# Deformable attention and a bottleneck block on one core: what the first and the last image do around the main loop

## The chip, the cores and the metric

The kernel runs on one core of a Trainium2 chip. The core has five engines that run side by side, each with its own list of instructions: TensorE (PE, matrix products), VectorE (DVE), ScalarE (ACT), GpSimd (POOL) and SyncE (SP, which here only issues transfers). They meet at semaphores. Data lies in SBUF (128 partitions), products go to PSUM, and 16 DMA engines move data from and to memory. Every number is float32. The metric is the device time of one execution in microseconds (us), as the median of several runs.

## What is computed

The input `x` holds 8 images of 512 channels and 64 by 64 pixels. Two layers follow each other, each behind a group norm over 32 groups and each added to its input.

Layer 0 is attention with deformed sampling. In the names of the reference, cut to what matters:

```
q   = w_q x                                   # 512 x 512, all 4096 pixels
t   = gelu(q[every 4th row and column] * w_off1 + b_off1)
off = tanh(w_off2 t) * 4                      # where to sample, per group of channels
kv_feats = bilinear samples of q at grid + off    # 16 x 16 = 256 positions
k, v = split(w_kv kv_feats)
out  = softmax(q k / 8) v                     # 8 heads of 64, 4096 queries, 256 keys
x    = x + w_out out + b_out
```

Layer 1 is a bottleneck: a 1x1 convolution from 512 to 32 channels, a depthwise 3x3 convolution of stride 2 (to 32 x 32), two dense layers over the 1024 pixels (to 256 and back), a depthwise 3x3 transposed convolution back to 64 x 64, and a 1x1 convolution to 512 channels, added to its input.

## The kernel before

**Tiles and buffers.** An image is 8 tiles (`NT`) of 512 pixels; a tile holds 4 blocks (`NCC`) of 128 channels. Two images lie in SBUF in turn. PSUM has eight banks of 128 x 512: two pairs in `ps_s` (tag `s`), two single banks that take turns in `ps_mm` (tag `mm`), and one bank each of tags `pa` and `pn` in `ps_a`. When a tile takes a bank, its first product waits until the last reader of the tile that had the bank is done. The order of instructions of each engine is the order in which the Python code issues them (a manual schedule); generators are advanced by hand, so that pieces of one image's work stand between pieces of another's.

**First images.** Image 0 is loaded, its statistics are taken (`norm_x`, L199), and `keep_up` (L1194) puts products on PE that nothing reads. `norm_q` turns the statistics into a scale and a shift: `group_stats` sums over groups with two small products (`gps`, L171, and `gpsb`, L180), each in a bank of `ps_mm`, VectorE and GpSimd finish the scale (L182, L183), and `normalise` (L212) applies it. The first tile's blocks go to VectorE (`t == 0`) or ScalarE, those of the second to GpSimd. `project_q` (L248) makes the query projection of one image, tile by tile, in the seven products of a Strassen-like scheme (L277): sums of weights are kept in the still unused buffers `wout` and `kt`, and the query is also turned into pixel-major form (`by_pixel`: transposes L326, copies L334 or L336, a write to memory on SP's queue, L337). The last tile's four transposes use the banks `pa`, `mm`, `pn`, `mm`. `activate` (L296) leaves gelu values for the offsets in the block `wout[:, 3]` and in a small tile. While image 0 is projected, image 1's statistics are taken between the pieces (L1210 to L1213), and its `group_stats` fall into the last tile of image 0 (L1212).

Then image 1's query projection runs beside the sampling of image 0 (`samples[0]`). `sample` (L421) begins with the offset products (L428, 16 small ones in a bank of `mm`) and a tanh (L437); VectorE works out the positions, GpSimd gathers rows of the pixel-major query (L523), and PE turns the weighted samples back to channels (L497). At the end of that come, in this order (L1222 to L1230):

```
while next(other) != LATE:
    pass
project_k(0, mqs.pop(0), wkv[0])
drain(other)
rest.pop(1)()
logits(*names[0])
next(samples[1])
load_wout()
project_v(0, wkv[1])
```

`project_k` makes the keys (L537, copied by ScalarE in L544), `drain(other)` is the four transposes of image 1's last tile, `rest.pop(1)` two maxima on VectorE (L288), `logits` the first products of query and keys with their exponentials (L584, L592), `next(samples[1])` image 1's offset products and tanh, `load_wout` the load of the output weights on SP's queue, which overwrites the block the offset products read, and `project_v` the values (L564, copied in L571). Until `logits` takes them, the four tiles `es4` hold the key and value weights of image 0 (`wkv`).

**Main loop.** A round `g` (L1231) is one pair of heads of one tile: the values weighted by the exponentials (`weighted_values`, L602), every second round the sum of the exponentials (L629), the logits of round `g + 1`, and, six rounds behind (`LAG`), one block of the output projection (`project_out`, L671). `fill` (L1237) advances the work beside it: the sampling and projections of the next image and layer 1 of the one before. From round 5 of image 0 on it also advances `samples[1]`. Reciprocals of the sums (`invert`, L642) are moved between partitions by SP (L648) and scale the result (`scale_two`, L651).

**Last image.** Behind the last round there is nothing to put beside, so layer 1 of image 7 runs alone (L1289 to L1316). `diag` holds diagonal matrices, made by ScalarE (L1297), with which PE computes some of the depthwise taps. `last_tile` (L755) takes the statistics and the 1x1 convolution (L737) block by block. `layer1` (L813) then goes from engine to engine: ScalarE and VectorE move the result to SBUF (L835, L837), the nine taps of the depthwise convolution go to VectorE (five, L881 and L883) and PE (four, L877), VectorE adds both (L879), two transposes (L889) with their copy (L892), the first dense layer (L900, L908, L914, L923), the second (L934, L947), the transposed convolution on PE (L984) beside VectorE (`upsample`), and the output products (L1007), to which the image is added (L1094); each 128 x 512 block is stored by SP (L1097).

Of the kernel before, what the change touches and what calls it, by code (L numbers as in the profile page):

```python
# [8 lines left out]
F32 = mybir.dt.float32  # L9
# [7 lines left out]
P = 128  # L17
B = 8
C = 512
NCC = C // P  # L20
# [29 lines left out]
def kernel(  # L50
# [111 lines left out]
    def group_stats(st, which, b):  # L162

        nm = f"{which}_{b}"
        mv = small.tile([P, NCC, 2], F32, tag="mv", name=f"mv{nm}")
        for cc in range(NCC):
            nc.vector.bn_aggr(mv[:, cc, :], st[:, cc].rearrange("p t s -> p (t s)"))
        mean, var = mv[:, :, 0], mv[:, :, 1]
        yield None
        gps = ps_mm.tile([P, TP], F32, tag="mm", name=f"gps{nm}")  # L170
        nc.tensor.matmul(gps[:, :NCC], cst[:, K_GRP : K_GRP + P], mean, start=True, stop=True)  # L171
        gs = small.tile([P, 2, NCC], F32, tag=f"gs{which}", name=f"gs{nm}")
        nc.vector.tensor_copy(gs[:, 0], gps[:, :NCC])
        dv = small.tile([P, NCC], F32, tag="dv", name=f"dv{nm}")
        nc.vector.tensor_sub(dv, mean, gs[:, 0])
        nc.vector.tensor_mul(dv, dv, dv)
        nc.vector.tensor_add(dv, dv, var)
        yield None
        gps2 = ps_mm.tile([P, TP], F32, tag="mm", name=f"gpsb{nm}")
        nc.tensor.matmul(gps2[:, :NCC], cst[:, K_GRP : K_GRP + P], dv, start=True, stop=True)  # L180
        ve = small.tile([P, NCC], F32, tag="ve", name=f"ve{nm}")
        nc.vector.tensor_scalar_add(ve, gps2[:, :NCC], EPS)  # L182
        nc.gpsimd.tensor_tensor(gs[:, 1], ve, nhalf, ALU.pow)  # L183
        return gs
# [22 lines left out]
    def norm_q(b, st, norms):  # L207
# [4 lines left out]
        def normalise(t, cc):  # L212
            xc, scale = x_tile(b, t)[:, cc, :], gs[:, 1, cc : cc + 1]
            if t == 1 or t == 0 and (b or cc < 2):
                (nc.vector, nc.gpsimd)[t].tensor_scalar(
                    xc, xc, gs[:, 0, cc : cc + 1], scale, ALU.subtract, ALU.mult
                )
            else:
                nc.scalar.activation(  # L219
                    xc, xc, AF.Identity, bias=shift[:, cc : cc + 1], scale=scale  # L220
                )
# [466 lines left out]
    def attention_max(b, t):  # L688

        qt = q_tile(b, t)  # L690
        for hp in range(NCC):
# [41 lines left out]
            nc.scalar.copy(qt[:, hp, :], pa)  # L733

    def convolve(b, py, cw, h, cc):
        for rb in range(4):
            nc.tensor.matmul(  # L737
                py[rb * CB : (rb + 1) * CB, :],
                cw[:, cc, :],
                out_tile(b, 2 * rb + h)[:, cc, :],  # L740
                start=(cc == 0),
                stop=(cc == NCC - 1),
            )
# [69 lines left out]
    def layer1(b, st, project, place, v, conv=None, diag=None):  # L813
# [13 lines left out]
        if conv:  # L827
            nc.vector.memset(y[:, :, 0:1], 0.0)
            nc.vector.memset(y[0:CB, 0:1, :], 0.0)
            py, pb = conv()  # L830
            nc.vector.tensor_sub(yb, col(V_CONVB), pb)
            for h in range(2):
# [39 lines left out]
        for k in range(9):  # L872
            ki, kj = divmod(k, 3)
            yk = y[:, ki : ki + 15 : 2, kj : kj + 63 : 2]
            w = col(V_DWW + k)
            if diag and k > 4:
                nc.tensor.matmul(pd, diag[V_DWW + k], yk, start=(k == 5), stop=(k == 8))  # L877
                if k == 8:
                    nc.vector.tensor_add(z, z, pd)  # L879
            elif k == 0:  # L880
                nc.vector.tensor_scalar(z3, yk, w, col(V_DWB), ALU.mult, ALU.add)  # L881
            else:
                nc.vector.scalar_tensor_tensor(z3, yk, w, z3, ALU.mult, ALU.add)  # L883
# [4 lines left out]
        for h in range(2):  # L888
            nc.tensor.transpose(pz[:, h * P : (h + 1) * P], z[:, h * P : (h + 1) * P], ident)  # L889
        o += NK  # L890
        zT = wflat[:, o : o + 2 * P].rearrange("p (h c) -> p h c", h=2)
# [5 lines left out]
        for k in range(8):  # L897
# [7 lines left out]
                stop=(k >= 4),  # L905
            )
        parts4 = z
        nc.scalar.copy(parts4, ph[:, : 2 * P])  # L908
# [4 lines left out]
        for oc in range(2):  # L913
# [5 lines left out]
                stop=True,  # L919
            )  # L920
        hT = small.tile([P, 2, CB], F32, tag="hT", name=f"hT_{b}")
        for oc in range(2):
# [7 lines left out]
        for n0, n, rbs in ((0, NK, 4), (NK, 32, 3)):  # L930
            for oc in range(2):
                for rb in range(rbs):
# [6 lines left out]
                        stop=(oc == 1),  # L939
                    )  # L940

        o += 2 * P
# [230 lines left out]
    with tc.manual_schedule():  # L1173
# [11 lines left out]
        load_weights_late()  # L1185
        st = new_stats(0, 0)
        drain(norm_x(0, st))

# [4 lines left out]

        def keep_up(n):  # L1194
            for _ in range(n):
                nc.tensor.matmul(idle, ident, x_tile(0, NT - 2)[:, 0, :], start=True, stop=True)

        keep_up(5)
        steps = norm_q(0, st, norms)
# [5 lines left out]
        drain(steps)  # L1205
        keep_up(2)

# [14 lines left out]
        while next(other) != LATE:  # L1222
            pass
        project_k(0, mqs.pop(0), wkv[0])
        drain(other)
        rest.pop(1)()
        logits(*names[0])
        next(samples[1])
        load_wout()
        project_v(0, wkv[1])  # L1230
        for g in range(len(names)):  # L1231
# [29 lines left out]
            else:  # L1261
                if summed:
                    invert(*names[g - 1])
                if g + 1 < len(names):
                    logits(*names[g + 1])
            if g % 2:
                scale_two()
# [26 lines left out]
        diag = {}  # L1294
        for i, w in enumerate([V_DWW + k for k in range(5, 9)] + [V_DEW + k for k in (0, 1, 2, 6, 7, 8)]):
            diag[w] = es4[i // 8][:, i // 4 % 2, i % 4 * P : (i % 4 + 1) * P]
# [138 lines left out]
```

## Time and profile before

| | |
|---|---|
| median of three runs | 3271.72 us (3270.57 to 3271.77) |
| the profiled execution's own time | 3273.27 us |
| its span, first to last instruction | 3271.5 us |
| mean granted clock of TensorE | 0.995 of full speed |
| busy of PE, DVE, ACT, POOL | 98%, 71%, 36%, 19% of the span |
| chain of work that ended last | PE 95%, DVE 3%, issue 1%, ACT 1% |
| keys of image 0 on PE (L537) | 261.3 to 268.4 us |
| first round of the main loop on PE (L602) | 285.34 us |
| last convolution of image 7 on PE (L737) | ends at 3223.6 us |
| first output block summed (L1094) | 3242.47 us |

An execution is recorded by the hardware profiler. Its page gives the busy time of every engine, the span in 40 slices with the clock that TensorE was granted, the chain of work that ended last, and the groups of instructions by line (L277 is line 277 of the kernel). The trace answers further questions: who waited for whom, instructions in order of time, and busy time by stretch. Matrix products are pipelined, and their ends are modelled.

### The profile page before, as it was taken

To read this page: it belongs to the slowest core of one execution; us is meant where nothing else is said; L and a number is where in the kernel's file an instruction comes from. 1 tells how busy PE (TensorE), PEld (TensorE's weight loads), DVE (VectorE), ACT (ScalarE), POOL (GpSimd) and SP (SyncE) were. 2 spreads that over 40 slices of the span, in tenths; PEclk is the share of its full clock that TensorE was granted. 3 is DMA by queue.
4 is the path that set the end of the run, shared out by engine and by line. 5 is a ranking of instruction groups with operands and counts; after the bars stand their busy time and mean duration, and the time that the engine had idled before them with its cause. 6 is when DMAs were issued, how large, how long until landed. Compare 5 with 4: busy or idle time off the path is not lost.

```text
span 3271.5 us, 46349 instructions
## 1 busy us (share of the span) xinstructions
PE 3216.1 (98%) x18270; PEld 1536.2 (47%) x18270; DVE 2322.9 (71%) x3779; ACT 1189.5 (36%) x1654; POOL 613.4 (19%) x579
## 2 busy tenths in 40 slices
PE   6999999999999999999999999999999999999997
PEld 5884223248332583326733277322763328533223
DVE  7884765787757777587775977669776697766665
ACT  2343333343333433344332443334433354332530
POOL 1130300130402304022040220303112040210301
PEclk9999999999999999999999999999999999999998
DMA  7232222672327523285332843238332572322714
GB/s 278 77 98 73 76 78 65 202 156 75 110 91 214 125 84 107 78 232 117 96 97 98 217 115 108 86 136 198 90 104 82 186 176 70 109 92 68 130 40 143
DMA packets 293858, 390.60 MB, mean 119 GB/s; under 512 B 18312, under 2 KB 157832, under 8 KB 293632
## 3 DMA queue, kind: packets, MB, share of 16 engines
q1 hardware_dynamic: 240352, 261.70, 24.6%
q0 software_dynamic: 53280, 125.86, 17.2%
q8 instruction: 145, 2.38, 0.3%
q14 instruction: 81, 0.66, 0.1%
HBM read 193.52 MB, written 192.94 MB: 118 GB/s over the span
## 4 chain that ended last, share of the span: by engine, by line
PE 95%; DVE 3%; issue 1%; ACT 1%; DMA 0%; POOL 0%; SPq 0%; ACTq 0%; DVEq 0%; POOLq 0%
PE pp L671 27%; PE pq L277 24%; PE ps L584 14%; PE pa L602 13%; PE pn L629 4%; PE pqt L326 4%; PE pv L564 2%; PE pk L537 2%; PE po L1007 2%; PE py L737 1%; DVE rn L642 1%; DVE image L1094 0%; PE po L428 0%; DVE st L199 0%; PE pu L934 0%
## 5 line engine op out<-in xcount | busy, mean ns | idle before, releaser
L671 PE MATMUL pp<-image,wout 128*64 128x512 f32 x3584 | 818.7, 599 | 0.0
L592 ACT ACTIVATE es<-ps 128x1024 f32<-128x1024 f32 x512 | 502.8, 1023 | 260.7 <-PE ps L584 210.3
L671 PEld LDWEIGHTS pp<-image,wout 128*64 128x64 f32 x3584 | 236.9, 136 | 540.9 <-issue 462.7
L602 PE MATMUL pa<-es,vt 128*64 128x512 f32 x2048 | 489.0, 598 | 1.7 <-ACT es L592 1.7
L523 POOL DMA_INDIRECT g<-qd,row x256 | 280.5, 1096 | 1053.5 <-DVE row L520 980.9
L277 PE MATMUL pq<-image,wbuf 128*128 128x256 f32 x2048 | 475.3, 380 | 1.4 <-ACT image L219 0.7
L584 PE MATMUL ps<-image,kt 64*64 64x512 f32 x3584 | 437.7, 602 | 0.3
L277 PEld LDWEIGHTS pq<-image,wbuf 128*128 128x128 f32 x2048 | 380.5, 191 | 55.0 <-issue 5.0
L680 DVE SCALAR_TENSOR_TENSOR image<-pp,vec,image 128x512 f32<-128x512 f32 x224 | 167.1, 746 | 332.8 <-PE pp L671 332.5
L609 ACT COPY image<-pa 128x512 f32<-128x512 f32 x224 | 131.9, 589 | 674.5 <-PE pa L602 674.5
L614 DVE TENSOR_TENSOR es<-es,es 128x1024 f32<-128x1024 f32 x256 | 310.9, 1214 | 72.4 <-PE pa L602 72.4
L602 PEld LDWEIGHTS pa<-es,vt 128*64 128x64 f32 x2048 | 137.4, 137 | 294.5 <-issue 274.6
L584 PEld LDWEIGHTS ps<-image,kt 64*64 64x64 f32 x3584 | 114.2, 132 | 308.1 <-issue 179.6
L336 ACT COPY qr<-pqt 128x512 f32<-128x512 f32 x224 | 131.0, 585 | 238.5 <-PE pqt L326 225.0
L642 DVE RECIPROCAL rn<-pn 128x512 f32<-128x512 f32 x63 | 211.3, 3353 | 7.8 <-PE pn L629 5.8
L655 DVE STREAM_SHUFFLE rb<-rn 128x512 f32<-128x512 f32 x252 | 184.4, 732 | 0.1
L183 POOL TENSOR_TENSOR gs<-ve,nhalf 128x4 f32<-128x4 f32 x15 | 16.1, 1070 | 893.6 <-DVE ve L182 893.6
L277 PE MATMUL pq<-es,es 128*128 128x256 f32 x768 | 181.5, 379 | 0.0
L1059 POOL DMA_DIRECT2D out_dram<-part x126 | 138.0, 1323 | 154.0 <-ACT part L1054 146.7
L199 DVE BATCH_NORM_STATS2 st<-image 128x6 f32<-128x512 f32 x256 | 159.1, 678 | 6.0 <-DMA image<-in_x_dram 6.0
L683 DVE BATCH_NORM_STATS2 st<-image 128x6 f32<-128x512 f32 x224 | 155.5, 694 | 7.7
L657 DVE TENSOR_TENSOR image<-image,rb 128x512 f32<-128x512 f32 x220 | 152.5, 693 | 7.6
(233 smaller groups left out, 3519.5 us busy)
## 6 DMA issues: line engine op xcount, KB each, us to landing
qd<-qr SPq DMA_DIRECT2D x256, 256.0 KB
image<-in_x_dram SPq DMA_DIRECT2D x112, 512.0 KB
out_dram<-image SPq DMA_DIRECT2D x49, 1024.0 KB
image<-in_x_dram POOLq DMA_DIRECT2D x48, 1024.0 KB, 10.1
out_dram<-part POOLq DMA_DIRECT2D x126, 256.0 KB, 7.3
image<-in_x_dram SPq DMA_DIRECT2D x16, 1024.0 KB
wbuf<-in_w_kvT_dram SPq DMA_DIRECT2D x14, 1024.0 KB
out_dram<-spare POOLq DMA_DIRECT2D x56, 256.0 KB, 7.7
```

The lines of the kernel that those rows point to most:

```text
L199: nc.vector.bn_stats(st[:, cc, t, :], x_tile(b, t)[:, cc, :])
L277: nc.tensor.matmul(bank[:, o * 2 * P : (o + 1) * 2 * P], w[:, k, o * P : (o + 1) * P], xh[:, k, :], start=(k == 0), stop=(k == 1),)
L523: nc.gpsimd.indirect_dma_start(held[-1][:, i, :, :].rearrange("p j d -> p (j d)"), None, qd[:, :], bass.IndirectOffsetOnAxis(ap=row[:, ky, ...
L584: nc.tensor.matmul(ps[k : k + DH, a, :], kt[r : r + DH, hp, kc * P + k : kc * P + k + DH], qt[r : r + DH, hp, :], start=True, stop=True,)
L592: nc.scalar.activation(e, ps, AF.Exp)
L602: nc.tensor.matmul(pa[a * DH : (a + 1) * DH, :], vt[:, kc, hd * DH : (hd + 1) * DH], es[kc][:, a, :], start=(kc == 0), stop=(kc == 1),)
L614: nc.vector.tensor_add(es[0], es[0], es[1])
L642: nc.vector.reciprocal(rn, denominators.pop((b, t)))
L655: nc.vector.stream_shuffle(rb, rn, [2 * (hp % 2) + hp // 2] * 32)
L671: nc.tensor.matmul(pp[r : r + DH, :], wout[:, hp, oc * P + r : oc * P + r + DH], ao[:, hp, :], start=(hp == 0), stop=(hp == NCC - 1),)
L680: nc.vector.scalar_tensor_tensor(xt[:, oc, :], pp, col(V_BOUT + oc), xt[:, oc, :], ALU.add, ALU.add)
L683: nc.vector.bn_stats(st[:, oc, t, :], xt[:, oc, :])
```

## The change

In the first images:

- One activation (Identity, on 4 columns of a small tile) is issued on ScalarE ahead of image 0's statistics, so the first load of ScalarE's function table comes with it.
- The two statistics products of image 1 go to the bank of tag `pn` in place of `mm`.
- `normalise` sends blocks 2 and 3 of image 1's first tile to ScalarE in place of VectorE, as it does for image 0.
- `project_v(0)` stands right behind `project_k(0)`; `next(samples[1])` and `load_wout()` move into round 0, behind the logits of round 1.

In the last image:

- A tap more of the depthwise convolution (`k = 4`) is computed by TensorE, which takes an eleventh diagonal.
- A new `keep_up` issues products of the identity with 256 columns of `wout` into a bank that nothing reads: three behind `last_tile`, one each behind the taps, the transposes, and the two steps of the first dense layer, two behind the second. The old function of that name is renamed `products`.

```diff
+        pool, tag = (ps_a, "pn") if (which, b) == (0, 1) else (ps_mm, "mm")
+        gps = pool.tile([P, TP], F32, tag=tag, name=f"gps{nm}")
...
+        gps2 = pool.tile([P, TP], F32, tag=tag, name=f"gpsb{nm}")
...
-            if t == 1 or t == 0 and (b or cc < 2):
+            if t == 1 or t == 0 and (b not in (0, 1) or cc < 2):
...
+    def keep_up(out, n):
+
+        for _ in range(n):
+            nc.tensor.matmul(out[:, :NK], ident, wout[:, 0, :NK], start=True, stop=True)
...
             py, pb = conv()
+            idle = ps_a.tile([P, TP], F32, tag="pa", name="idle_last")
+            keep_up(idle, 3)
...
-            if diag and k > 4:
-                nc.tensor.matmul(pd, diag[V_DWW + k], yk, start=(k == 5), stop=(k == 8))
+            if diag and k > 3:
+                nc.tensor.matmul(pd, diag[V_DWW + k], yk, start=(k == 4), stop=(k == 8))
                 if k == 8:
                     nc.vector.tensor_add(z, z, pd)
+                    keep_up(idle, 1)
...
             nc.tensor.transpose(pz[:, h * P : (h + 1) * P], z[:, h * P : (h + 1) * P], ident)
+        if diag:
+            keep_up(idle, 1)
...
+        if diag:
+            keep_up(idle, 1)
         parts4 = z
...
+        if diag:
+            keep_up(idle, 1)
         hT = small.tile([P, 2, CB], F32, tag="hT", name=f"hT_{b}")
...
+        if diag:
+            keep_up(idle, 2)
...
         st = new_stats(0, 0)
+        ve0 = small.tile([P, NCC], F32, tag="ve", name="ve_table")
+
+        nc.scalar.activation(ve0, nhalf, AF.Identity, bias=nhalf[:, 0:1], scale=nhalf[:, 0:1])
         drain(norm_x(0, st))
...
         project_k(0, mqs.pop(0), wkv[0])
+        project_v(0, wkv[1])
         drain(other)
         rest.pop(1)()
         logits(*names[0])
-        next(samples[1])
-        load_wout()
-        project_v(0, wkv[1])
...
                 if g + 1 < len(names):
                     logits(*names[g + 1])
+                if g == 0:
+                    next(samples[1])
+                    load_wout()
...
-        for i, w in enumerate([V_DWW + k for k in range(5, 9)] + [V_DEW + k for k in (0, 1, 2, 6, 7, 8)]):
+        for i, w in enumerate([V_DWW + k for k in range(4, 9)] + [V_DEW + k for k in (0, 1, 2, 6, 7, 8)]):
```

More of the change, by code (lines that the diff above doesn't have):

```diff
@@ L169, in group_stats @@
         yield None
-        gps = ps_mm.tile([P, TP], F32, tag="mm", name=f"gps{nm}")
+        pool, tag = (ps_a, "pn") if (which, b) == (0, 1) else (ps_mm, "mm")
+        gps = pool.tile([P, TP], F32, tag=tag, name=f"gps{nm}")
         nc.tensor.matmul(gps[:, :NCC], cst[:, K_GRP : K_GRP + P], mean, start=True, stop=True)
@@ L178, in group_stats @@
         yield None
-        gps2 = ps_mm.tile([P, TP], F32, tag="mm", name=f"gpsb{nm}")
+        gps2 = pool.tile([P, TP], F32, tag=tag, name=f"gpsb{nm}")
         nc.tensor.matmul(gps2[:, :NCC], cst[:, K_GRP : K_GRP + P], dv, start=True, stop=True)
@@ L1192, with products @@
         idle = ps_a.tile([P, TP], F32, tag="pa", name="idle")
-        def keep_up(n):
+        def products(n):
             for _ in range(n):
                 nc.tensor.matmul(idle, ident, x_tile(0, NT - 2)[:, 0, :], start=True, stop=True)
-        keep_up(5)
+        products(5)
         steps = norm_q(0, st, norms)
@@ L1205 @@
         drain(steps)
-        keep_up(2)
+        products(2)
         st = new_stats(0, 1)
```

## The prediction

> **What bounds the kernel now.** The page comes first.
>
> ```profile
> PE 3216.1 (98%) x18270; PEld 1536.2 (47%) x18270; DVE 2322.9 (71%) x3779; ACT 1189.5 (36%) x1654; POOL 613.4 (19%) x579
> PEclk9999999999999999999999999999999999999998
> ```
>
> TensorE (PE) is busy for 98% of the span, and nearly always at full clock. The change cannot shorten the middle (a step of an image after the first takes as long as before), so what it is worth lies where PE waits or runs at half clock. The view of waits, for PE alone, lists these places; those that the change touches are
>
> ```profile
> PE pd L877 <- DVE wbuf L835: 1.6, 1, 1.6
> PE pz L889 <- DVE wbuf L879: 1.6, 1, 1.6
> PE pq L277 <- DVE image L390: 1.4, 1, 1.4
> PE pv L564 <- DVE qr L334: 1.2, 1, 1.2
> PE pv L984 <- DVE wbuf L947: 1.0, 1, 1.0
> PE pq L277 <- ACT image L219: 0.7, 1, 0.7
> ```
>
> (total, times, longest, in us). All lie before 290 us or after 3220 us. The order of time there shows what stands in front of each (start, length, then what the engine had idled for):
>
> ```profile
> 33.32 1.28 ACT L219 ACT_TABLE_LOAD   x1 [33.32 <-DVE shift L228]
> 35.48 2.27 PE L277 MATMUL pq<-image,wbuf 128*128 128x256 f32 x8 [0.69 <-ACT image L219]
> ...
> 144.14 1.99 PE L277 MATMUL pq<-image,wout 128*128 128x256 f32 x8 [1.38 <-DVE image L390]
> ...
> 275.26 10.15 PE L564 MATMUL pv<-es,image 128*128 128x512 f32 x16 [1.16 <-DVE qr L334]
> 285.34 1.94 PE L602 MATMUL pa<-es,vt 128*64 128x512 f32 x8
> 289.44 1.99 PE L602 MATMUL pa<-es,vt 128*64 128x512 f32 x8 [0.28 <-ACT es L592]
> ...
> 3233.20 2.14 PE L934 MATMUL pu<-w,hT 128*32 128x256 f32 x28 [0.34 <-DVE hT L923]
> 3236.36 5.01 PE L984 MATMUL pv<-wbuf,es 128*128 128x128 f32 x24 [1.01 <-DVE wbuf L947]
> ```
>
> The reader is to see that the value products (L564) take 10.15 us for 16 instructions, 0.63 each, though 512 columns elsewhere take 0.43. Stretches of time say why (the eighth figure group is the clock):
>
> ```profile
> 278.00:280.00 2.00, 2.00 (x4) 0.97 (x3) 0.00 (x0) 0.00 (x0) 0.00 (x0) 0.50 0.99 331
> 3227.07:3230.48 3.41, 1.33 (x16) 0.62 (x18) 2.06 (x5) 0.00 (x0) 0.00 (x0) 1.00 0.00 0
> 3233.00:3234.00 1.00, 0.80 (x8) 0.40 (x12) 0.42 (x4) 0.00 (x0) 0.00 (x0) 0.50 0.00 0
> 3250.00:3251.00 1.00, 1.00 (x4) 0.23 (x4) 0.92 (x5) 0.00 (x0) 1.00 (x1) 1.00 1.03 383
> ```
>
> From the mean clock of the bins at their edges, it is halved from 274.5 to 281.4 and from 3230.5 to 3240.7. The last line shows the end: from 3244 on the stores fill the DMA engines at some 380 GB/s, so the end follows the moment at which the first output is ready.
>
> [...] The window ahead of the second fall is the second line above: 1.33 of 3.41 us busy, 39%. The one before it (3223.65 to 3227.07) had 1.83 us, 54%, and stayed at full clock; one with 2.39 us of 3.40 (3233.9) did not bring it back, one with 3.15 (322.3) did. [...]
>
> **Part 1, table ahead.** One activation on 4 columns is added on an idle ACT (its first work now is at 33.32) and the load of 1.28 us moves to about 1 us. It writes the small `ve` tile, next written at 30: no cover is needed. Normalised channel blocks 2 and 3 are then ready at 33.3 + 0.76 = 34.1 and 34.9, not at 35.4 and 36.1. PE's first eight products issue until 34.53; the second eight (8 x 0.216) follow at once, and those of the third (L366) issue at 36.3, not at 37.5; their operand (L268, 0.69) is ready at 35.6. From there on PE is busy without a gap to 142, so 1.2 us stay: **-1.2**.
>
> **Part 2, statistics in the bank apart.** The product at 144.14 (L394) waits for a bank that L390 reads until 144.09, because the statistics took the other `mm` turn. With them in `pn`, it finds the bank whose reader L368 ended at 136.8, and follows the statistics' product at 142.75. L395 then starts at 144.75, not 146.17, the transposes of the last tile at 145.5, not 146.92, image 1 at 147.3. What is late next: the scale from GpSimd at 145.38, and L215's first two at 145.5 to 146.8, in time for image 1's products at 147.3. Blocks 2 and 3 of tile 0 go from VectorE (2 x 0.68) to ACT (2 x 0.81, ending at 148.6), ahead of PE's need at 149.0; ACT idles there. VectorE's copies of the transposes (L334), queued behind them, come earlier too. The new users of `pn` are read out by 144.15, before the transposes want it: no wait. PE has no gap from there to 274: **-1.4**.
>
> **Part 3, values behind keys, offset products in round 0.** Now: keys end at 268.3; transposes 2.0; logits 1.95; offset products 1.95 (16 small ones); wait 1.16; values 10.15; round 0 from 285.34; round 1 from 289.44. Then: values at 268.3 right behind the keys, in banks that ACT's key copies (0.38 each, L544) have left, 16 x 0.43 = 6.9, to 275.2; transposes to 277.1 (ACT's value copies, 0.58, free their banks by 276.0; the exponential's table load follows, ending at 277.2 before its first input at 278.3); logits to 279.1; 0.3 for the first exponential; round 0 at 279.4, logits of round 1 to 283.2, offset products to 285.1, which cover the wait for the exponential; round 1 at 285.2: 4.2 earlier. Of VectorE: the last two copies (L334) wait for the write of the first (2.61 us in the chain, as now), to 280.8; the two maxima (2.33) to 283.1; the first sum of exponentials (1.23), now at 286.53, to 284.4, wanted at 288. The SP queue: the load of `wout` now waits for the offset products; behind it stand the four copies of the reciprocal at about 305, twenty us later. It moves 1 MB, some 3 us at 300 GB/s, and its first use (L671) is at 317 now, so near 310 then. Tanh on ACT stands at 285.2 where ACT idles. **-4.2**, of which half is the clock, and holds to the end since the rounds run one behind another. I take the clock to stay up in round 0: an equal run of offset products at 152.27, where products before and behind it were dense, left it at 1.00. Bounds: nothing, or one window at half clock, +1.7.
>
> **Part 4, the last image.** The tap on TensorE takes one L883 off VectorE (0.50) and adds two products of 0.216 to the eight of L877: these now end at 3227.4, then at 3227.8, as L879 starts at 3227.9. -0.5. The eleventh copy of a diagonal (0.30 on ACT at 3187.6) is covered by 36 us of idle ACT. The unread products are pairs of 0.216, so 0.43 each at full clock: three (1.3) in the gap of 1.60 ahead of L877, one each in the gaps behind L877 (1.56), L889 (0.52), L900 (0.47), L914 (0.34), two (0.86) in 1.01. Only the one in 0.34 is over, by 0.1. The emptiest window then, from 3227.6, holds 0.45 + 0.45 + 0.9 + 0.55 = 2.35 us of counted work, 69% against the 54% that sufficed: the clock stays. At full clock the 24 products of L984 cost 0.118 each (spacing of loads of 128 columns in L326: 1.88 for 16), so 2.83 for 5.01: -2.0 with the lag; L934 1.2 for 2.14: -0.9; L900 and L914 -0.45 each. Sum with the tap -4.3, less 0.1: **-4.2**. If the clock falls all the same, the products cost up to 0.35 + 0.4 + 0.5 + 0.7 over their gaps, and the part gives between -0.5 and +1.7.
>
> **Sum.** -1.2 - 1.4 - 4.2 - 4.2 = -11.0 on the profiled 3273.27 us (span 3271.5 and 1.8 around it), so 3262.3; that run lies 1.55 above the median 3271.72, so as a median **3260.7**. The three runs spread over 1.2 us; what can't be told from no change is 0.2%, 6.5 us, so faster means below 3265.2. The place at 319 to 323 (PE idle, then 3.4 us at half clock) stays, but its phase against the windows shifts: +-1.5.
>
> **Rivals.** (a) The clock falls at the end anyway. For: gaps remain, and pad products are short; against: 69%. Then part 4 gives between -0.5 and +1.7, near +0.5: -6.3, 3265.4. (b) A wait takes the place of those removed at the front, for instance the scale from GpSimd at 145.38, or one fallen window in round 0: parts 1 and 2 half, part 3 -2.5: -8.0, at worst -6; 3263.7. (c) Slower: the clock falls at the offset products, now among rounds that hold waits, and stays down until the output projection. Each round needs 3.8 us of PE at full clock and 7.6 at half, in 4.15: five rounds add some 17 us: 3278. It decides when more than 22 us are spent at half clock. Against it: at half clock PE no longer waits, and full windows brought the clock back at 281.4 and 325.7. That an edit does nothing is likeliest for part 1, and is in (b).
>
> **How the numbers follow.** Main case 0.76, (a) 0.12, (b) 0.09, (c) 0.03. The range takes the windows' phase, one fallen window and most of (a): 3257.5 to 3265.5. Faster: the main case but 0.01, 0.03 of (a), 0.07 of (b): 0.85. Slower: (c), 0.03. The rest, 0.12, is the same.
>
> **What would show it.** No table load at 33; no wait on L390 at 143; L564 in 6.9 us directly behind L537, with the clock at 1.00 from 265 to 300; L984 in about 3.0 us and the clock at 1.00 from 3220 to 3235; the first output sum (L1094) about 11 us earlier; and distances between steps of the middle images unchanged. I am wrong if the rounds of image 0 show half clock, if L984 still takes 5 us, or if a new wait of over 1 us stands in front of L277 or L602.

## The result and the profile after

The changed kernel takes 3261.83 us (median of 8 runs, 3261.64 to 3262.84). The kernel before, in the same series, takes 3271.25 us (8 runs, 3270.57 to 3274.38). The ratio is 0.997 (95%: 0.9961 to 0.998). In a later series it was 3261.5 against 3272.14 us, 0.9967 (0.9955 to 0.9979). So the change is faster by 9.4 us in one series and 10.6 us in the other, some 0.3%, and a median of 3260.7 us had been forecast. Between the two profiled executions the span goes from 3271.5 to 3259.9 us, 11.6 less.

Lines of the kernel after are numbered higher: L277 is now L279, L390 L392, L564 L566, L602 L604, L984 L1002, L1094 L1112. The page of the kernel after, busy time and clock:

```profile
PE 3212.8 (99%) x18290; PEld 1536.5 (47%) x18290; DVE 2320.5 (71%) x3776; ACT 1193.5 (37%) x1658; POOL 612.8 (19%) x579
...
PEclk9999999999999999999999999999999999999999
```

PE has 20 instructions more than before and is busy for 3.3 us less: products at half clock have gone. The waits of PE after (total, times, longest, in us):

```profile
PE pp L673 <- DVE spare L659: 3.0, 2, 2.6
...
PE gpsb L182 <- DVE dv L179: 0.8, 1, 0.8
PE pqt L328 <- DVE image L397: 0.7, 1, 0.7
PE pq L279 <- DVE image L217: 0.6, 1, 0.6
```

Of the six waits that the prediction showed, none is left. The 0.6 us ahead of the first products, for VectorE's block, stood there before as well. Behind the first load, the largest wait left is at the output projection of image 0, and the change does not touch it. The order of time after (start, length, idle time ahead):

```profile
0.74 1.28 ACT L1207 ACT_TABLE_LOAD   x1 [0.74 <-PEq L1447]
...
33.87 4.12 PE L279 MATMUL pq<-image,wbuf 128*128 128x256 f32 x16 [0.59 <-DVE image L217]
...
142.85 1.97 PE L279 MATMUL pq<-image,wout 128*128 128x256 f32 x8
...
266.97 7.03 PE L566 MATMUL pv<-es,image 128*128 128x512 f32 x16
...
278.07 1.99 PE L604 MATMUL pa<-es,vt 128*64 128x512 f32 x8 [0.28 <-ACT es L594]
...
281.87 1.05 PE L430 MATMUL po<-vec,wout 128*128 128x4 f32 x8
...
283.75 1.94 PE L604 MATMUL pa<-es,vt 128*64 128x512 f32 x8
...
3218.12 2.60 PE L886 MATMUL pd<-wbuf,es 128*128 128x256 f32 x10
...
3224.89 1.19 PE L950 MATMUL pu<-w,hT 128*32 128x256 f32 x28
...
3227.20 2.94 PE L1002 MATMUL pv<-wbuf,es 128*128 128x128 f32 x24
```

The first sixteen products run as one block, where eight and then a pause had been. The 16 value products take 7.03 us for 10.15, the 24 of the transposed convolution 2.94 for 5.01. Two stretches of the kernel after (length, then busy us and instructions of PE, PEld, DVE, ACT, POOL, then the clock). The time of the first had been at half clock before, and so had the work of the second, the second dense layer and the transposed convolution:

```profile
278.00:280.00 2.00, 1.93 (x9) 0.40 (x10) 1.84 (x3) 0.93 (x2) 0.00 (x0) 1.00 0.32 95
3224.60:3228.00 3.40, 3.34 (x41) 2.21 (x40) 2.18 (x10) 0.00 (x0) 0.00 (x0) 1.00 0.00 0
```

The shift of the second profile against the first can be followed from mark to mark. Each row is the start of the named work; the last column is what was gained since the row above.

| | before | after | shift | gained here |
|---|---|---|---|---|
| scale products of image 0 (`gps`) | 28.38 | 29.94 | +1.56 | +1.56 |
| first projection products | 32.40 | 33.87 | +1.47 | -0.09 |
| third product group of tile 0 | 37.59 | 37.82 | +0.23 | **-1.24** |
| L394's products, last tile of image 0 | 144.14 | 142.85 | -1.29 | **-1.52** |
| keys of image 0 | 261.33 | 260.02 | -1.31 | -0.02 |
| third round, weighted values | 293.60 | 287.85 | -5.75 | **-4.44** |
| last group of the last convolution | 3223.04 | 3215.92 | -7.12 | -1.37 |
| first output sum | 3242.47 | 3231.25 | -11.22 | **-4.10** |
| span | 3271.5 | 3259.9 | -11.6 | -0.4 |

### The profile page after: what moved, and what is told of

Same layout as the page of the kernel before. It is cut to its first block, busy times and chain, and to the rows that moved or that the text cites. A ratio compares the mean times of both kernels' runs of the same rounds, so it can differ in the third digit from the quotient of the medians.

```text
span 3259.9 us, 46393 instructions
## 1 busy us (share of the span) xinstructions
PE 3212.8 (99%) x18290; PEld 1536.5 (47%) x18290; DVE 2320.5 (71%) x3776; ACT 1193.5 (37%) x1658; POOL 612.8 (19%) x579
## 4 chain that ended last, share of the span: by engine, by line
PE 95%; DVE 3%; issue 1%; ACT 0%; POOL 0%; SPq 0%; DMA 0%; ACTq 0%; DVEq 0%; POOLq 0%
PE pp L673 28%; PE pq L279 24%; PE ps L586 14%; PE pa L604 13%; PE pn L631 4%; PE pqt L328 4%; PE pk L539 2%; PE pv L566 2%; PE po L1025 2%; PE py L744 2%; DVE rn L644 1%; PE po L430 0%; DVE image L1112 0%; DVE st L201 0%; PE pf L499 0%
## 5 line engine op out<-in xcount | busy, mean ns | idle before, releaser
L604 PE MATMUL pa<-es,vt 128*64 128x512 f32 x2048 | 488.5, 598 | 1.7 <-ACT es L594 1.7
L279 PE MATMUL pq<-image,wbuf 128*128 128x256 f32 x2048 | 474.7, 380 | 0.7 <-DVE image L217 0.6
L279 PEld LDWEIGHTS pq<-image,wbuf 128*128 128x128 f32 x2048 | 380.7, 191 | 53.6 <-issue 5.0
L604 PEld LDWEIGHTS pa<-es,vt 128*64 128x64 f32 x2048 | 137.1, 136 | 292.8 <-issue 272.3
L279 PE MATMUL pq<-es,es 128*128 128x256 f32 x768 | 181.5, 379 | 0.0
L221 ACT ACTIVATE image<-image,shift,gs 128x512 f32<-128x512 f32 x196 | 156.8, 813 | 36.0 <-DVE shift L230 36.0
```

The costliest lines, as they stand in the source:

```text
L221: nc.scalar.activation(xc, xc, AF.Identity, bias=shift[:, cc : cc + 1], scale=scale)
L279: nc.tensor.matmul(bank[:, o * 2 * P : (o + 1) * 2 * P], w[:, k, o * P : (o + 1) * P], xh[:, k, :], start=(k == 0), stop=(k == 1),)
L604: nc.tensor.matmul(pa[a * DH : (a + 1) * DH, :], vt[:, kc, hd * DH : (hd + 1) * DH], es[kc][:, a, :], start=(kc == 0), stop=(kc == 1),)
```

## The experiments

All kernels are the kernel before or the kernel after with the edit shown. "Distance" below is the time between two marks of the table within one profile, so that shifts from earlier stages drop out. A "window" is a step of 3.41 us: the shortest stretch at half clock in the trace of the kernel before lasts that long (322.32 to 325.73 us), and its other stretches between two changes of the clock last whole multiples of it (the last section has them). The 95% interval of each ratio is in brackets.

**The table load alone** (before, with this):

```diff
+        ve0 = small.tile([P, NCC], F32, tag="ve", name="ve_table")
+        nc.scalar.activation(ve0, nhalf, AF.Identity, bias=nhalf[:, 0:1], scale=nhalf[:, 0:1])
```

> The kernel before with the activation ahead of the statistics and nothing else. Theory of the prediction: the third group of products (L366) stands 1.2 us nearer to the first, the first statistics of image 0 begin at 5.9 us as before, and the median falls by 1.2 us (3270.0). Rival: the table load at the very start holds up the first loads; then the first statistics begin at 6.3 us as in the changed kernel's profile, and 0.4 of the gain is lost (3270.4). Second rival: the start is set by when the clock comes up, and the median stays within 0.5 us of before.

Measured: 3269.25 us (13 runs) against 3272.16 (49 runs), 0.9992 (0.9983 to 1.0). From the first projection products to the third group it is 3.95 us for 5.19, so 1.24 less, as in the changed kernel. The median is 2.9 us lower, more than twice what was expected, but the interval reaches to no change; what this edit does is read from the distance. The first statistics begin at 6.02 us, against 5.92 and 6.27 in two profiles of the kernel before: the load does not delay them. The value products took 8.83 us here, not 10.15: they were hit by the same fall of the clock, but for one window (274.7 to 278.1) in place of two (274.5 to 281.4). The edit does not touch that place, so it differs from run to run.

**Statistics back in the old bank** (after, with this):

```diff
-        pool, tag = (ps_a, "pn") if (which, b) == (0, 1) else (ps_mm, "mm")
+        pool, tag = ps_mm, "mm"
```

> The changed kernel with the statistics products of image 1 in the turn of two banks as before; blocks 2 and 3 of image 1's first tile stay with ScalarE. Theory: the wait of 1.4 us in front of the last product of image 0's query projection is back, and the offset products of image 0 stand 1.4 to 1.5 us later against the third product group of the start; median 1.4 us above the changed kernel (3263.2). Rival (moving the two blocks to ScalarE is what brought image 1 forward): under 0.5 us.

Measured: 3264.61 us (8 runs) against 3272.81 (14 runs), 0.9975 (0.9965 to 0.9986), so 2.8 to 3.1 us above the two medians of the changed kernel. From the third group to L394's products it is 106.55 us, exactly the distance before, against 105.03 after. The wait is back in the order of time:

```profile
143.98 1.99 PE L279 MATMUL pq<-image,wout 128*128 128x256 f32 x8 [1.38 <-DVE image L392]
```

So the bank brings the 1.52 us. For what the medians show above that, this profile has a candidate: from the third round to the last convolution it loses 1.9 us against the one after, with half clock at the output projection of image 0. Whether most runs of this kernel do so isn't known. ScalarE still takes the two blocks in this kernel, and nothing comes of that alone.

**Values behind keys, and nothing else** (before, with this):

```diff
         project_k(0, mqs.pop(0), wkv[0])
+        project_v(0, wkv[1])
         drain(other)
...
         load_wout()
-        project_v(0, wkv[1])
```

> The kernel before with the values behind the keys; offset products and the load of the output weights stay ahead of the main loop. Theory (the gain of this part is the value products at full clock and without the wait for a bank): the 16 value products take 7.0 us, round 2 (third group of weighted values) starts 4.2 to 4.5 us earlier, the median falls by 4 us, as much as with the offset products in round 0. Rival (it takes both, since the offset products leave TensorE light ahead of round 0): under 2 us.

Measured: 3269.02 us (21 runs) against 3272.16 (49), 0.9991 (0.9984 to 0.9997). From the keys to the third round 27.82 us, against 32.27 before and 27.83 after: one of the two moves gives the whole gain of part 3 in the profile. The median falls by 3.1 us.

**Offset products in round 0, and nothing else** (before, with this):

```diff
         logits(*names[0])
-        next(samples[1])
-        load_wout()
         project_v(0, wkv[1])
...
                 if g + 1 < len(names):
                     logits(*names[g + 1])
+                if g == 0:
+                    next(samples[1])
+                    load_wout()
```

> The kernel before with only the offset products and the load of the output weights moved into round 0; the values stay behind the logits of round 0. Theory: the values then wait for their bank from 272.2 to 275.2 us with nothing before it, the clock falls as before, the value products take some 10 us, and the median stays within 0.7 us of before. Rival (the offset products in front of the values are what makes the clock fall): values in about 7 us and a median 2.5 us or more below before.

Measured: 3268.87 us (21 runs) against 3272.16 (49), 0.9988 (0.9982 to 0.9995), so 3.3 us less; the distance is 27.69 us. I had expected the wait ahead of the values to stay, and it did not. In order of time:

```profile
271.86 1.95 PE L584 MATMUL ps<-spare,kt 64*64 64x512 f32 x16
273.73 7.21 PE L564 MATMUL pv<-es,image 128*128 128x512 f32 x16
```

Without the offset products between them, the values take the other turn of the two `mm` banks, which is read out by then. So this move alone gives the whole gain too. The gains of the two moves are the same gain, not two halves.

**Offset products where they were, in another bank** (before, with this). This takes away the bank turn and leaves the order as it was:

```diff
-        po = ps_mm.tile([P, TP], F32, tag="mm", name=f"po_{b}")
+        pool, tag = (ps_a, "pa") if b == 1 else (ps_mm, "mm")
+        po = pool.tile([P, TP], F32, tag=tag, name=f"po_{b}")
```

> The kernel before in its own order, but image 1's offset products go to the bank `pa`, so the values no longer inherit the bank whose copy waits for a write. Theory (the clock falls because the offset products hardly count as work): the wait of 1.2 us in front of the values goes, the clock still falls, and the 16 value products take 9 to 10 us; the third group of weighted values stands 31 us behind the keys in place of 32.2; median 1 us below before. Rival (it is the 1.2 us of idling that makes the clock fall): values in 7 us, 28 us behind the keys, as with either move alone; median 3 us or more below before.

Measured: 3269.01 us (21 runs) against 3272.14 (42), 0.999 (0.9984 to 0.9997), so 3.1 us less; the distance is 27.93 us.

```profile
273.32 1.05 PE L429 MATMUL po<-vec,wout 128*128 128x4 f32 x8
274.24 1.03 PE L429 MATMUL po<-vec,qs 128*128 128x4 f32 x8
275.13 7.11 PE L565 MATMUL pv<-es,image 128*128 128x512 f32 x16
```

The sixteen small products stand just ahead of the values, as in the kernel before, and the clock does not fall: the values take 7.11 us for 10.15. So in this run their place alone does not cost the clock, which had been my theory for it; the fall came only with the wait of 1.16 us behind them. That a wait of this length is enough by itself is not shown. What speaks against it is the wait of 1.38 us ahead of L394's products: it tipped the clock in none of the eight profiles that have it. There nearly all other work of PE has 128 columns or more; here 16 products of 4 columns stand next to the wait. Whether these weigh as little as an idle PE stays unsettled: with the wait gone, any stretch of 3.41 us here still holds 1.6 us of full-width work, and before it was 1.05 us in the stretch that ended with the fall (the 272.15 at which the offset products begin, less 271.1).

The distance of 32.27 us is not what every run has. In the four profiles of kernels with the old order and the old bank (before, before once more, table alone, tap alone) it is 32.27, 32.18, 30.94 and 30.94: the clock fell in all four, in the first two for two windows, in the others for one. That fits medians that fall by 3.1 to 3.3 us and not by 4.4.

A single turn from bank to bank costs 4.4 us in the profile before: 1.16 is the wait itself, and the rest is work at half clock behind it.

**No unread products** (after, without all calls of the new `keep_up`):

```diff
-            idle = ps_a.tile([P, TP], F32, tag="pa", name="idle_last")
-            keep_up(idle, 3)
...
-                    keep_up(idle, 1)
...
-            keep_up(idle, 2)
```

> The changed kernel without the products that nothing reads in the last image; the fifth tap stays on TensorE. Theory: the clock falls at a window's edge between the taps and the first dense layer and stays down for two or three windows; the 24 products of the transposed convolution take 4.4 to 5.0 us in place of 2.94, and the first output sum stands 18.9 us behind the last convolution's last product, in place of 15.3 (19.4 in the kernel before). Median 3.5 us above the changed kernel (3265.3). Rival (the fall there is the luck of a phase): 15.3 to 16, and a median within 1 us of the changed kernel.

Measured: 3263.31 us (6 runs) against 3272.81 (14), 0.9969 (0.9957 to 0.9981). From the last convolution to the first output sum it is 16.67 us, against 15.33 after and 19.43 before. The clock fell, but for one window, and the sum was 1.3 us later, not 3.5 as I had expected. The median is 1.5 to 1.8 us above the changed kernel's. Two of the six runs took 3261.26 and 3260.36 us, no more than the changed kernel, and the other four 3263.14 to 3263.72; so the fall may be absent in some runs. In the old ending it was no matter of luck: in all six profiles of kernels that have it, the clock fell there for three windows, and the distance is 19.35 to 19.43 us. The stretches around the fall without the unread products:

```profile
3220.47:3223.88 3.41, 2.19 (x21) 0.82 (x20) 1.49 (x4) 0.06 (x1) 0.00 (x0) 1.00 0.00 0
3223.88:3227.30 3.42, 1.82 (x32) 1.25 (x32) 1.33 (x6) 0.32 (x1) 0.00 (x0) 1.00 0.02 5
3227.30:3230.72 3.42, 3.29 (x15) 3.30 (x16) 1.90 (x7) 0.27 (x1) 0.00 (x0) 0.50 0.00 0
```

**No tap more on TensorE** (after, with `k > 4`, `start=(k == 5)` and `range(5, 9)` as before):

```diff
-            if diag and k > 3:
-                nc.tensor.matmul(pd, diag[V_DWW + k], yk, start=(k == 4), stop=(k == 8))
+            if diag and k > 4:
+                nc.tensor.matmul(pd, diag[V_DWW + k], yk, start=(k == 5), stop=(k == 8))
```

> The changed kernel with four taps on TensorE and five on VectorE as before; the unread products stay. Theory: VectorE ends one tap of 0.50 us later, and the first output sum stands 15.8 us behind the last convolution in place of 15.3; median 0.5 us above the changed kernel. Rival (VectorE waits for TensorE's taps anyway, with the unread products ahead of them): no difference, the wait shows in front of the sum of both.

Measured: 3262.09 us (6 runs) against 3272.81 (14), 0.9968 (0.9956 to 0.998). The same distance is 15.85 us, 0.52 more than after, as expected; the medians differ by 0.3 to 0.6 us, which these runs can't tell from nothing.

**The tap, and no unread products, in the kernel before** (with `range(4, 9)` in the list of diagonals):

```diff
-            if diag and k > 4:
-                nc.tensor.matmul(pd, diag[V_DWW + k], yk, start=(k == 5), stop=(k == 8))
+            if diag and k > 3:
+                nc.tensor.matmul(pd, diag[V_DWW + k], yk, start=(k == 4), stop=(k == 8))
```

> The kernel before with five taps on TensorE, without the unread products and without every other part. From the run without the unread products: the longer run of taps and the earlier first dense layer carry the clock past the edge at which it fell, and it falls one window later if at all: the first output sum stands 16.7 us or less behind the last convolution, in place of 19.4; median 2.7 us below before. The theory of the prediction (the taps alone give 0.50 us, the clock falls as before): 18.9 us and a median 0.5 us below before.

Measured: 3268.11 us (21 runs) against 3272.14 (42), 0.9988 (0.9981 to 0.9995), so 4.0 us less. The distance is 15.12 us, 4.31 less than before and 0.2 less than in the changed kernel. The lines show full speed:

```profile
3226.79 0.44 PE L889 MATMUL pz<-ident,wbuf 128*128 128x128 f32 x2 [0.57 <-DVE wbuf L879]
...
3230.28 1.19 PE L934 MATMUL pu<-w,hT 128*32 128x256 f32 x28 [0.34 <-DVE hT L923]
3232.48 2.94 PE L984 MATMUL pv<-wbuf,es 128*128 128x128 f32 x24 [1.01 <-DVE wbuf L947]
```

The idle time behind the taps is 0.57 us, and it was 1.56: PE's part has become longer by two products and VectorE's shorter by one tap. So in this run the tap does what the unread products do. Over all stretches of 3.41 us that begin in steps of 0.2 us in the last image up to the first output sum, the emptiest has 1.33 us of PE busy before, 1.81 with the tap, 2.20 with the unread products, and 3.17 with both. The run without the unread products has the tap too, and there the clock fell; here it held. What made the difference isn't shown; where the windows lay may be part of it. With the unread products the clock holds up to the first output sum in all six profiles that have them. The distance is 0.2 us longer with them than with the tap alone. Behind that sum the clock falls in these profiles too, in two of them with output products still to come. That costs nothing that can be seen: from the first sum to the end it is 28.5 to 29.2 us in every profile.

**The kernel before, once more, unchanged:**

> The kernel before, unchanged, profiled once more. The profile shown of it belonged to an execution of 3273.27 us, 2.0 us over its median of 3271.25. If those 2 us are the phase of the clock's windows (theory), this profile shows the same instructions with other stretches at half clock: start of the values (L564) up to 10.15 us or less, the place of 322 to 326 us with or without a fall, and a span near 3269.5. If they are something else (rival), the stretches at half clock are where they were and the span differs elsewhere.

Measured: one run of 3273.53 us, span 3271.6, with half clock in the same places (274.7 to 281.6, 3230.7 to 3240.9 and, by the lengths of the products there, 322.5 to 325.9). By its own terms the theory missed. But the run could not decide: the windows' edges lie within 0.2 us of where they lay in the first profile (274.7 us for 274.5, with the keys at 261.7 for 261.3), so this is nearly the same draw again. The profiles with the table or the tap alone have the same instructions at the values and half clock for 3.4 us there, not 6.8; so what is lost there does change from run to run, as the theory says. The 49 runs of the kernel before in that series lie between 3268.57 and 3273.88 us, and both profiled executions belong to the upper part.

**The kernel after, once more, unchanged:**

> The changed kernel, unchanged, in one series with the runs of this call. Theory: median 3261.8 and a spread of about 1 us, since no place is left in it where the clock falls by the luck of a phase except the gap ahead of the output projection; the kernel before spreads over 4 to 5 us. Rival (the two medians known so far belong to different series and the gain is really smaller): under 9 us below before.

Measured: 3261.5 us (6 runs, 3260.9 to 3262.45). The changed kernel is not only faster, its runs lie closer: 1.2 us from first to last in 8 runs and 1.55 in 6, where the kernel before has 3.8 us in 8 runs (and 5.3 in 49).

**Beyond the change: image 1's positions earlier.** The chain of the kernel after, at the largest wait that is left, shows what it hangs on:

```profile
309.78 0.69 DVE spare L659
310.48 0.11 DVE pos L441
...
314.32 0.72 DVE rb L657
...
317.31 1.08 PE pp L673 x4
```

Between two of the multiplications that the output projection waits for, VectorE works out where image 1 is sampled (some twenty small steps, 310.48 to 314.3). After, with this, those steps come in the rounds ahead:

```diff
                 if g == 0:
                     next(samples[1])
                     load_wout()
+                if g in (1, 3, 4):
+                    next(samples[1])
```

> The changed kernel, and beyond it the position steps of image 1's sampling (some 3.9 us of small VectorE work that stands between the first and the second scaling of the results, ahead of the output projection) are issued in rounds 1, 3 and 4, where VectorE idles. Theory: the chain from the reciprocal to the third output product loses these 3.9 us, TensorE's gap of 3.5 us in front of the output projection shrinks to about 0.5, and with it goes the risk of a clock fall there: median 3.4 us or more below the changed kernel (3258.4). Rival (the work delays the sums of exponentials, or a gather that now starts a round earlier takes VectorE's time): rounds 1 to 5 grow, and the median stays within 1 us of the changed kernel.

Measured: 3257.7 us (5 runs, 3257.11 to 3258.48) against 3272.81 (14), 0.9954 (0.9941 to 0.9968). It beats both kernels, the changed one by about 4 us. The sixteen products run in one block and the wait is gone:

```profile
310.17 3.65 PE L673 MATMUL pp<-spare,wout 128*64 128x512 f32 x16
```

The two waits had been 3.0 us together, and between profiles without a fall at this place the time from the third round to the last convolution is 3.0 us shorter. The rest of the 4 us fits the clock: five profiles are of kernels with the change to the first images, whole or but for the bank, and with this wait. In three of them the clock fell here, and from the four products behind the second wait to the next projection it is 6.0 to 6.3 us, where it is 4.6 at full clock. The rival, that rounds 1 to 5 grow, is not seen.

**With seven start products on an earlier tile besides** (the kernel above, with this):

```diff
-                nc.tensor.matmul(idle, ident, x_tile(0, NT - 2)[:, 0, :], start=True, stop=True)
+                nc.tensor.matmul(idle, ident, x_tile(0, NT - 3)[:, 0, :], start=True, stop=True)
...
-        products(5)
+        products(7)
```

> The kernel with the positions early, and at the start seven in place of five products on a tile that lands one tile earlier. Theory: the products at half clock no longer stand in front of the first statistics product, which then starts at 28.4 to 28.8 us in every run, in place of 28.4 to 30.1; median 0.8 us below the kernel with the positions early (3256.9). Rival (the clock falls again ahead of the first projection products, or the two further products cost what the earlier start gives): 3257.5 or more, with the first projection products at half clock.

Measured: 3257.59 us (5 runs) against 3272.14 (42), 0.9954 (0.9941 to 0.9968). `gps` begins at 28.93 us, later than the 28.4 to 28.8 that I had expected, and against 28.75 in the profile of the kernel above. The median is 0.1 us below that kernel's in another series: no gain that these runs can tell. The clock does not fall ahead of the first projection products, as the rival had it; they take as long as in the kernel above.

## Why the prediction was right, point by point

**The whole.** The sum of -11.0 us was made between profiled executions, and they differ by 11.6. The four parts were forecast at -1.2, -1.4, -4.2 and -4.2 and measured at -1.24, -1.52, -4.44 and -4.10. The median was forecast at 3260.7 and is 3261.83, or 3261.5. What was off by 1.1 us is the last step of the sum, from profile to median. I took 1.55 us off because the profiled run lay that far above its median. Very likely it lay there because it lost more to half clock than most (two windows at the values, where two other profiles have one), and just that loss is what the change removes. The profiled run after lies at 3261.64, 0.2 below its median. Had the surplus been left to the gain, the median would have been forecast at 3262.3.

**Part 1, -1.2: right.** It is -1.24, and the table alone shows it. **Part 2, -1.4: right.** It is -1.52, and goes when the bank is given back.

**Part 3, -4.2: right in size for that profile (-4.44), and in its time table.** On the scale of the kernel before (shift 1.31 up to the keys), round 0 begins at 279.38 and round 1 at 285.06, where 279.4 and 285.2 were forecast. The values take 7.03 us for the 6.9. What the prediction didn't see is that either of the two moves would have done. It named the banks of the values as a condition, but not that the wait ahead of them was a matter of bank turns alone. It also said that half of the gain is the clock; the wait is 1.16 of 4.4, so the clock is nearer three quarters. And it took the two windows at half clock as given, where some runs have one.

**Part 4, -4.2: right in sum (-4.10), wrong in its split.** The step that failed is the "-0.5" for the tap, with the rest of the part put down to the unread products. The working looked only at the tap's own time. That it closes 1 us of the idle time behind the taps, in the emptiest window, was not carried into the clock. With it alone the part gave -4.31 in its profile; without the unread products, but with the whole change to the first images, the tap gave -2.76. The 0.5 us is right where the clock holds anyway (no tap: +0.52). The clock held as forecast, but the reason given for it, that 69% of a window is more than the 54% behind which it had stayed at full speed, was my estimate from one stretch. It takes PE's busy share as the measure, and by that share the runs can't be put in order (see below). It also leaves the two transposes out, an assumption that no run here shows. Even so the share was worked out too low: without them the emptiest stretch has 2.9 us, not 2.35.

**What had no term in the sum.** In the profile after, the clock came up at 28.5 us in place of 25.4 (from there on the start products follow each other in 0.43 us, and in 0.85 before), so the start products took longer, 7.39 us for 6.04; they also began 0.4 us later. That puts `gps` 1.56 us later. In the other profiles `gps` lies between 28.38 and 30.05, whether the front is changed or not, so this is the draw of one run. Against it stands the place at 319 to 323, which the prediction left at plus or minus 1.5: -1.37. In the profile after the clock held there, and in the three variants with the same instructions there it did not, so this too is the draw of one run. Both terms nearly cancel; that the sum of profiles came within 0.6 us is in part luck.

**The rivals.** (a) The clock falls at the end anyway: not seen with the unread products. Without them it was real, in the profile taken, at one window and 1.3 us. (b) A wait takes the place: none. The scale from GpSimd, its likeliest place, is ready at 145.62 in the profile after, and the products of image 1 begin at 147.51. (c) The clock falls in the rounds: it did not, and the offset products between rounds 0 and 1 stand at full clock. What the profile had to show is there in each point: no load at 33 us, no wait on L392, L566 directly behind the keys, L1002 in 2.94 us, and the first output sum 11.2 us earlier, where about 11 were forecast.

**What stays open.** What in a window decides whether the clock falls behind it. By PE's busy share alone the windows can't be put in an order. One with 1.82 of 3.42 us (53%) ended in a fall in the run without unread products, and in the kernel before one with the same 1.82 us, just ahead of the emptiest, did not. At the output projection of image 0, the emptiest window has 0.79 to 1.44 us in the ten profiles in which the clock fell, and 1.41 and 1.64 us in the two of the changed kernel, in which it held. In the kernel before the stretch from 271.1 to 274.5, with 3.00 of 3.40 us, ended in a fall, its products being of 4 columns in large part. Whether transposes weigh as other products do, no run here shows by itself. How often the clock falls in each place is seen from a dozen profiles at most: always at the old ending (six) and at the values in the old order (four), in ten of twelve at the output projection.

## What to carry to other kernels

A short wait of PE can cost several times its length, when work behind it runs at half clock; here 1.16 us cost 4.4, with the clock at half for 6.83 us. Not every wait does: one of 1.38 us among dense work did in none of eight profiles. So the first thing to find is the wait, the second how much work stands around it (the runs here don't show how much is enough), and the third what then runs at half clock. Such a loss can be removed by any of several edits, each of which gives all of it, so their gains are not to be added: the values' move, the offset products' move and another bank gave 4.3 to 4.6 us each in their profiles and 3.1 to 3.3 in the medians, and the two moves together 4.4 in the profile. Where the surplus of a profiled run over the median is itself the loss that an edit removes, it belongs to the gain and is not to be subtracted again. And one more profile is one more draw: it can land on the same phase as the first, as that of the kernel before did, with the edges of the windows 0.2 us from where they had been.

## What the runs showed of the hardware

The clock fell behind windows that were far from idle. In the kernel before, PE is busy for 1.33 us (39%) of the 3.41 ahead of the fall at 3230.47 us, and for 3.00 of the 3.40 ahead of the one at 274.53. In the run without unread products it is busy for 1.82 us (53%) of the 3.42 ahead of the fall at 3227.30.

In the trace of the kernel before, the clock stands at 1.00 or at 0.50 of full speed, and the changes lie whole windows apart. From the fall at 274.53 us on they are at 281.36, 322.32, 325.73, 3230.47, 3240.71 and 3261.19 us. Between them are 6.83, 40.96, 3.41, 2904.74, 10.24 and 20.48 us, which is 2, 12, 1, 851, 3 and 6 times 3.4133. Read from stretches of 1 us, half clock lasts 3.42 and 10.24 us with the table alone, and 6.84 and 10.24 us in the kernel before once more. From run to run the edges mostly lie elsewhere: in the two profiles of the changed kernel the clock first comes up at 28.5 and at 27.0 us, where the start products go from 0.85 us each to 0.43 in the one and from two in 1 us to four in the other. That the kernel before spreads over 3.8 us in 8 runs, while the changed one, without most of its falls, spreads over 1.2 in as many, goes with this: with the same instructions at the values, two profiles had half clock for two windows and two for one. Of the five profiles of the changed kernel and its near variants, two had the place at the output projection at full clock and three at half, with the same instructions in it.
